# Six routed sequences' first products in pairs, as quarter products

## The chip, the cores and the metric

One core of a Trainium2 chip runs the kernel, as one program. The metric is the device time of one execution in microseconds, the median over several runs.

## The reference, cut to what matters

`x` has 8 sequences of 128 rows and 512 columns. Layer 0 adds an adapter product with a small LoRA mixture to it. Layer 1 computes attention over a paged cache (32 query heads, 8 key heads, head size 128, 512 cached keys and 128 new ones a sequence) and passes its output `y` through a routed product:

```python
scores = (y @ Wq_w.T) @ keys.T                    # 64 experts
top_vals, top_idx = top_k(scores, 16)
gate = scatter(softmax(top_vals))                 # 0 for the other 48
z = (y @ A_w.T).reshape(..., 64, 8)
x = x + ((z * gate[..., None]).reshape(..., 512) @ B_w.T) * SCALING
```

The change is in `y @ A_w.T` (512 x 512 a sequence), the scores and the gate.

## The kernel before, in words

Everything is fp32. Attention runs as 64 units (`NU = 64`; a unit is one key head with its four query heads `h` = 0 to 3, for one sequence), in the calls `iteration(u)`, u = 1 to 66, written out in order: the order in the code is each engine's order. The call `iteration(u)` handles several units at different stages: scores (PE, `s`, L439/L442) and exponential of unit u (DVE masks and takes the maximum, L452; ACT exponentiates, L463; DVE reciprocal, L468; POOL normalizes, L469; DVE transposes blocks, L474, L425 for the rotated queries and keys), a trip of these blocks through DRAM (`exchange_out`, `exchange_in`, tiles `px`, `pT`, `qkb`), the queries of unit u + 1 (ACT, `qkT`, L973), norms and rotation of unit u + 3 (ACT L311, POOL L315/L317, DVE L343), `values` of unit u - 2 (PE, `o`, L986), and `output` of unit u - 3 (PE, `y`, L1111 or L1124, after ACT's copy `oT`, L1009, which `evict_o` makes at the top of the call). DVE adds `y` up (L1180) and makes masks (L409).

After a sequence's last unit its routed product follows, in three steps. `f_turn` transposes `y` on PE (`ftp`, L858) and copies it (ACT, `yT`, L860). `f_project` (L867) multiplies it with the router and the weights side by side in `fw_t["sa"]`: `sz` (PE name `fr`) takes the 64 router columns and the first 256 of `A_w`, `z` (`fz`) the other 256, four 128-row chunks each; a call in fp32 is two instructions of the profile. The first lies in PSUM bank "q", the second in bank "kv". `f_gate` (L878 to L900) copies the scores out, finds the sixteen largest on DVE, exponentiates on ACT (L890), normalizes, and multiplies `z` by the gates from PSUM into `zg`. Sequences 0 to 6 do this at u = 59 to 65:

```python
LAST = {NU - 5 + b: b for b in range(B - 1)}
```

`f_turn` is called at h = 2 (h = 1 at u = 61, the top of the call from u = 64 on), `f_project` and `f_gate` at the end of the call, ahead of `values`; from u = 64 on `values` goes first (`ahead`). The gated `z` of sequences 0 to 5 is then block-transposed on DVE (`z_blocks`, L372), written to DRAM and read back turned (`z_exchange`, SP's queue, one sequence an iteration), copied (`z_turn`, ACT L393), and combined in pairs by POOL (`z_sums`). The second products, with `B_w`, are already made in pairs as seven quarter products (Winograd's form) behind the loop: `f_products`, PE `op` L1466, DVE additions L1477, and `f_store`. POOL makes the quarter sums of `B_w` in `f_quarters` (L934 to L937) at u = 64. `f_fold` (L850) folds weight columns at u = 59. `f_load_x` loads the rows of `x` that the output is added to. Sequence 7 is done behind the loop, and so are the last `z` turns.

PSUM has one bank each for "q", "kv", "o" and "y" and two double banks for scores.

Of the kernel before, what the change touches and what calls it, by code (L numbers as in the profile page):

```python
# [16 lines left out]
P = 128  # L17
# [41 lines left out]
def adaln_ffn_kernel(  # L59
# [816 lines left out]
    def f_gate(b, sz, z, sb, psum):  # L876
        sc = sb("sc", [P, E1])
        nc.vector.tensor_copy(sc, sz[:, :E1])  # L878
# [18 lines left out]
        nc.vector.tensor_scalar(wf, wf, den, SC1, ALU.mult, ALU.mult)  # L897
        zg = sb("zg", [P, DM])
# [29 lines left out]
    def f_quarters():  # L928
        b = fw_t["b"]
        q11, q12, q21, q22 = (b[:, 2 * i : 2 * i + 2, j * HN : (j + 1) * HN] for i in (0, 1) for j in (0, 1))  # L930
        room = [wo_t[:, i].rearrange("p (t c n) -> p t c n", t=2, c=2) for i in (3, 6)]
        t3, t2, t4, t1 = (room[i // 2][:, i % 2] for i in range(4))
        tt = nc.gpsimd.tensor_tensor
        tt(t3, q22, q12, ALU.subtract)  # L934
        tt(t2, t3, q11, ALU.add)
        tt(t4, q21, t2, ALU.subtract)
        tt(t1, q12, q11, ALU.subtract)  # L937
        fw_t["q"] = [q11, q21, q22, t4, t1, t2, t3]

    def z_sums(p):  # L940
        a, b = zT_t.pop(2 * p), zT_t.pop(2 * p + 1)
        at = p % 3 * 2 * DM
        room = spare[:, at : at + 2 * DM].rearrange("p (k c s) -> p k c s", k=4, c=2)
# [3 lines left out]
        tt(s1, a21, a22, ALU.add)  # L947
        tt(s2, s1, a11, ALU.subtract)
        tt(s4, a12, s2, ALU.subtract)
        tt(s3, a11, a21, ALU.subtract)  # L950
        zs_t[p] = [a11, a12, s4, a22, s1, s2, s3]
# [3 lines left out]
    with ExitStack() as l1:  # L955
# [276 lines left out]
        LAST = {NU - 5 + b: b for b in range(B - 1)}  # L1232
        yT_t, room_t = {}, {}

        def rooms():
            w = wp.tile([P, 7 * 2 * HW], F32, tag="wqkv", name="rooms", bufs=GH)
            at = [0]

            def part(size):
                at[0] += size  # L1240
                return w[:, at[0] - size : at[0]]

            for b in range(B - 1):
                room_t["zg", b] = part(DM)
            for i in range(2):
                room_t["yT", i] = part(DM)
                room_t["small", i] = part(352)

        def room(b):
# [9 lines left out]
            def psum(n, shape):  # L1259
                late = n == "tp" and b >= 5  # L1260
# [32 lines left out]

# [139 lines left out]
    with ExitStack() as l2:  # L1433
# [13 lines left out]
        def room4(z):  # L1447
            t = kvp.tile([P, 2 * DM], F32, tag="kt", name=f"fzT_{z}")
            return [t[:, i * DM : (i + 1) * DM].rearrange("p (c s) -> p c s", c=NC) for i in range(2)]

        M1, M2, M3, M4, M5, M6, M7 = range(7)
# [10 lines left out]
        def f_products(p, t, *which):  # L1462
            halves = [t[:, i * HN : (i + 1) * HN] for i in range(len(which))]
            for ps, n in zip(halves, which):
                for c in range(2):
                    nc.tensor.matmul(  # L1466
                        out=ps,
                        lhsT=zs_t[p][n][:, c, :],
                        rhs=fw_t["q"][n][:, c, :],
                        start=(c == 0),  # L1470
                        stop=(c == 1),
                    )
# [27 lines left out]
        end(0)  # L1500
        z_sums(2)
# [102 lines left out]
```

## Time and profile before

| | us |
|---|---|
| three runs | 1200.83, 1204.02, 1205.5 |
| median | 1204.02 |
| the profiled execution | 1200.24 |
| its span | 1198.5 |
| unit 59 starts (first `s`) | 1049.68 |
| units 60, 61, 62, 63 | 1066.35, 1086.23, 1100.89, 1120.69 |
| calls 64 and 65 and 66 start on PE | 1137.9, 1149.6, 1161.8 |
| first second product (`op`) | 1165.3 |
| last matmul ends | 1194.8 |

The granted TensorE clock of the execution is 1.000. In a row of the profile the engine is followed by the line of the kernel, the operation, the tile written and the tiles read (buffer numbers left out), shapes, and in brackets how long the engine idled before and what released it. PE is TensorE's matmuls, PEld its weight loads, DVE VectorE, ACT ScalarE, POOL GpSimd, SP SyncE.

### The profile page before, as it was taken

The page shows a single profiled execution, that of the slowest core. Times are in us where ns is not written, and L with a number is a line of the kernel's source. Part 1 is how long each engine was busy: PE and PEld are TensorE (multiplying, and loading weights), DVE is VectorE, ACT ScalarE, POOL GpSimd, SP SyncE. Part 2 cuts the span into 40 slices and gives each one's busy share as a digit, 9 for nine tenths or more (in the row PEclk, how much of TensorE's full clock was granted, in tenths as well). Part 3 has the DMA queues.
Part 4 walks back from the last instruction along what each step waited for, and adds up shares of the span by engine and source line. Part 5 has one row for each costly group of instructions (what it writes and reads, how often), then busy time and mean ns, then how long its engine had stood idle before and what let it go on. Part 6 is the DMA issues. An engine that isn't in the chain of part 4 may idle for free.

```text
span 1198.5 us, 16919 instructions
## 1 busy us (share of the span) xinstructions
PE 1189.8 (99%) x4196; PEld 723.0 (60%) x4196; DVE 927.0 (77%) x2122; ACT 504.2 (42%) x1457; POOL 755.1 (63%) x848
## 2 busy tenths in 40 slices
PE   9999999999999999999999999999999999999998
PEld 7666555565555556555556555555655555655557
DVE  2557788787888887878887787879888888887727
ACT  1345544443444444444444444444444444443310
POOL 3544779778845776678656685687657684653311
PEclk9999999999999999999999999999999999999999
DMA  8823787888888979898789978897889887888751
GB/s 317 304 83 114 249 247 242 261 274 261 263 255 254 315 236 284 262 292 287 246 257 285 291 232 283 286 287 251 285 237 308 266 252 246 277 281 243 230 176 71
DMA packets 205446, 302.34 MB, mean 252 GB/s; under 512 B 84771, under 2 KB 119332, under 8 KB 204324
## 3 DMA queue, kind: packets, MB, share of 16 engines
q1 hardware_dynamic: 170164, 196.29, 53.6%
q10 hardware_dynamic: 18864, 52.57, 13.7%
q0 software_dynamic: 16320, 52.40, 12.5%
q8 instruction: 34, 0.56, 0.2%
q14 instruction: 64, 0.52, 0.1%
HBM read 185.44 MB, written 115.74 MB: 251 GB/s over the span
## 4 chain that ended last, share of the span: by engine, by line
PE 91%; DVE 2%; POOL 2%; DMA 2%; ACT 1%; issue 1%; SPq 0%; ACTq 0%; DVEq 0%; POOLq 0%
PE o L986 20%; PE p L262 19%; PE s L439 17%; PE y L1111 13%; PE s L442 4%; PE p L295 3%; PE cp L627 2%; PE y L1124 2%; PE bp L649 2%; PE fr L867 1%; PE op L1466 1%; PE fz L867 1%; DVE xo L1477 1%; DMA qkb<-px 1%; ACT sq L311 1%
## 5 line engine op out<-in xcount | busy, mean ns | idle before, releaser
L463 ACT ACTIVATE p<-p,low 128x640 f32<-128x640 f32 x256 | 211.8, 828 | 430.6 <-DVE den L468 270.3
L469 POOL TENSOR_SCALAR p<-p,den 128x640 f32<-128x640 f32 x256 | 210.5, 823 | 231.9 <-DVE den L468 231.1
L452 DVE CUSTOM_DVE_ANT_0 p<-s,mask,rs 128x640 f32<-128x640 f32 x256 | 222.5, 879 | 86.9 <-PE s L442 85.2
L262 PE MATMUL p<-wqkv,xo 128*128 128x384 f32 x784 | 281.0, 487 | 0.1
L439 PE MATMUL s<-kt,qkT 128*128 128x512 f32 x504 | 258.1, 593 | 2.7 <-ACT oT L1009 1.9
L986 PE MATMUL o<-pT,vt 128*128 128x512 f32 x512 | 230.2, 592 | 0.0
L474 DVE STREAM_TRANSPOSE pb<-p 128x640 f32<-128x640 f32 x248 | 204.7, 826 | 21.5 <-POOL p L469 21.3
L1111 PE MATMUL y<-wo,oT 128*128 128x256 f32 x784 | 206.5, 380 | 0.5 <-DVE yp L1198 0.4
L262 PEld LDWEIGHTS p<-wqkv,xo 128*128 128x128 f32 x784 | 148.3, 190 | 69.2 <-POOL wqkv L163 0.9
L442 PEld LDWEIGHTS s<-qkT 128*128 128x128 f32 x504 | 95.8, 190 | 120.5 <-issue 120.5
L203 POOL DMA_INDIRECT vt<-in_vc,vrow x128 | 137.9, 1077 | 41.4 <-issue 31.5
L986 PEld LDWEIGHTS o<-pT,vt 128*128 128x128 f32 x512 | 97.2, 190 | 107.9 <-issue 92.8
L439 PEld LDWEIGHTS s<-kt,qkT 128*128 128x128 f32 x504 | 94.8, 190 | 74.6 <-issue 30.7
L1111 PEld LDWEIGHTS y<-wo,oT 128*128 128x128 f32 x784 | 131.8, 191 | 9.4 <-PE s L442 0.6
L311 ACT ACTIVATE sq<-c 128x128 f32<-128x128 f32 x320 | 98.8, 309 | 9.7 <-DVE oT L474 1.4
L442 PE MATMUL s<-qkT 128*128 128x128 f32 x504 | 96.8, 274 | 0.0
L317 POOL TENSOR_TENSOR rs<-ss,mhalf 128x5 f32<-128x5 f32 x64 | 82.4, 1287 | 5.3
L1009 ACT COPY oT<-o 128x512 f32<-128x512 f32 x64 | 37.4, 585 | 103.8 <-PE o L986 79.9
L315 POOL TENSOR_SCALAR ss<-ss,eps 128x5 f32<-128x5 f32 x64 | 24.7, 387 | 72.4 <-ACT sq L311 72.4
L986 PE MATMUL o<-pT,vn 128*128 128x512 f32 x128 | 65.4, 592 | 0.0
L265 DVE TENSOR_TENSOR c<-c,p 128x384 f32<-128x384 f32 x84 | 44.9, 534 | 24.1 <-PE p L262 23.8
L425 DVE STREAM_TRANSPOSE pb<-ca 128x640 f32<-128x640 f32 x60 | 50.1, 836 | 16.5 <-DMA kt<-in_kc 12.6
(255 smaller groups left out, 1481.2 us busy)
## 6 DMA issues: line engine op xcount, KB each, us to landing
pT<-px SPq DMA_DIRECT2D x64, 1280.0 KB
px<-pb SPq DMA_DIRECT2D x120, 400.0 KB
px<-pb ACTq DMA_DIRECT2D x120, 400.0 KB
qkb<-px SPq DMA_DIRECT2D x60, 320.0 KB
kt<-in_kc SPq DMA_DIRECT2D x512, 32.0 KB
wqkv<-in_wqkv POOLq DMA_DIRECT2D x32, 384.0 KB, 5.1
wo<-in_wo POOLq DMA_DIRECT2D x17, 512.0 KB, 7.7
yd<-yp POOLq DMA_DIRECT2D x12, 512.0 KB, 8.8
```

The lines of the kernel that those rows point to most:

```text
L203: nc.gpsimd.indirect_dma_start(out=kv_t[step][1][:, c, :], out_offset=None, in_=vc, in_offset=bass.IndirectOffsetOnAxis(ap=vrow[:, hf, at ...
L262: nc.tensor.matmul(out=ps, lhsT=xo[:, pr, x, c, :], rhs=w[:, c, :], start=(c == 0), stop=(c == 1))
L311: nc.scalar.activation(sq, cs[:, at : at + D], AF.Square, accum_out=ss[:, h : h + 1])
L317: nc.gpsimd.tensor_tensor(rs, ss, mhalf, ALU.pow)
L439: nc.tensor.matmul(out=s[:, :L], lhsT=qkT[:, h, :], rhs=kt[:, :, g % GH, :], start=True, stop=True)
L442: nc.tensor.matmul(out=s[:, L:NK], lhsT=qkT[:, h, :], rhs=qkT[:, REP, :], start=True, stop=True)
L452: nc.vector.tensor_tensor_reduce(out=p, in0=s_t.pop((u, h))[:, :NK], in1=mask_t[st], scale=rs_t[u][:, h : h + 1], scalar=BIG, op0=ALU.add, ...
L463: nc.scalar.activation(p, p, AF.Exp, bias=low, scale=-1.0, accum_out=den)
L469: nc.gpsimd.tensor_scalar(p_t[u, h], p_t[u, h], den, 1.0, ALU.mult, ALU.mult)
L474: nc.vector.transpose(pb_t[u][:, :, h * w : (h + 1) * w].rearrange("p i (j a) -> p j i a", a=32), p_t.pop((u, h)).rearrange("p (j i a) -> ...
L986: nc.tensor.matmul(out=o, lhsT=vt[:, c, j * D : (j + 1) * D] if c < LC else vn_t.pop(u), rhs=pT[:, c], start=(c == 0), stop=(c == LC),)
L1111: nc.tensor.matmul(out=y_t["y"][:, half * HN : (half + 1) * HN], lhsT=part(key)[:, i * S : (i + 1) * S], rhs=wo_t[:, slot(w, key[0] // (B ...
```

## The change

Sequences 0 to 5 are taken in the pairs (0,1), (2,3), (4,5). The 256 x 512 rows of a pair (two sequences' `yT`) times `A_w` become seven products M1 to M7 of quarters, each 128 rows by 256 columns with two 128-row chunks. The quarter sums of `A_w` are made once by four POOL steps of 128x512 (`qa_steps`, u = 59 and 60), those of `yT` by four POOL steps of 128x256 a pair (`f_step`). M1 and M2, which need only the even sequence, are made at the end of u = 59, 62, 64 (`FIRST`) and carry 64 router columns each, whose sum is the even sequence's scores; ACT copies their `z` part out (`m1`, `m2`) and the even gate is made. The rest is made at u = 61, 63, 65 (`REST`): M4, which carries router columns that hold one half of the odd sequence's scores, and a 64-column product `own_r` with the other half into the same bank, at h = 3; then M5, M6, M3, M7 at the end. M1 and M5 with M6 use bank "q"; M2, M4 with `own_r`, and M3 with M7 use bank "kv". At u = 62, 64, 66 (`GATED`) `f_add` puts the products together with six DVE adds of 256 columns, `f_mult` multiplies both sequences' `z` by the gates (two DVE steps of 128x512), and the pair's blocks are transposed; the exchange goes out one iteration later and back in after another. `f_turn` of the even sequences moves to behind h = 3 (u = 59, 62) or the top (u = 64), of the odd ones to h = 1 or the top (u = 65). Sequence 6 keeps the old form and moves from u = 65 to u = 66. `values` goes first from u = 63 on. The quarter sums of `B_w` use other rooms, `f_load_x` moves to u = 66 and behind the loop, and the last two `z` turns follow `end(0)`.

```diff
-    def f_gate(b, sz, z, sb, psum):
+    def f_scores(r, sb):
         sc = sb("sc", [P, E1])
-        nc.vector.tensor_copy(sc, sz[:, :E1])
+        nc.vector.tensor_copy(sc, r[0])
+        for more in r[1:]:
+            nc.vector.tensor_tensor(sc, sc, more, ALU.add)
+        return sc
...
+    def quarters_of(m, *rooms):
+        q11, q12, q21, q22 = (m[:, 2 * i : 2 * i + 2, j * HN : (j + 1) * HN] for i in (0, 1) for j in (0, 1))
+        t3, t2, t4, t1 = rooms
         tt = nc.gpsimd.tensor_tensor
...
+        steps = [
+            lambda: tt(t3, q22, q12, ALU.subtract),
+            lambda: tt(t2, t3, q11, ALU.add),
+            lambda: tt(t4, q21, t2, ALU.subtract),
+            lambda: tt(t1, q12, q11, ALU.subtract),
+        ]
+        return [q11, q21, q22, t4, t1, t2, t3], steps
...
+    def sums_of(a, b, room):
+        room = room.rearrange("p (k c s) -> p k c s", k=4, c=2)
         s1, s2, s3, s4 = (room[:, i] for i in range(4))
         a11, a12, a21, a22 = a[:, :2], a[:, 2:], b[:, :2], b[:, 2:]
...
+        steps = [
+            lambda: tt(s1, a21, a22, ALU.add),
+            lambda: tt(s2, s1, a11, ALU.subtract),
+            lambda: tt(s4, a12, s2, ALU.subtract),
+            lambda: tt(s3, a11, a21, ALU.subtract),
+        ]
+        return [a11, a12, s4, a22, s1, s2, s3], steps
...
+    def quarter_products(t, left, right, *which):
+        halves = []
+        at = 0
+        for n in which:
+            halves.append(t[:, at : at + right[n].shape[2]])
+            at += right[n].shape[2]
+        for ps, n in zip(halves, which):
+            for c in range(2):
+                nc.tensor.matmul(
+                    out=ps,
+                    lhsT=left[n][:, c, :],
+                    rhs=right[n][:, c, :],
+                    start=(c == 0),
+                    stop=(c == 1),
+                )
+        return halves
...
-        LAST = {NU - 5 + b: b for b in range(B - 1)}
+        LAST = {NU + 2: B - 2}
+        FIRST = {NU - 5: 0, NU - 2: 1, NU: 2}
+        REST = {NU - 3: 0, NU - 1: 1, NU + 1: 2}
+        GATED = {NU - 2: 0, NU: 1, NU + 2: 2}
...
-        def z_blocks(b):
-            if 0 <= b < TURNED:
-                turn_blocks(zg_t[b], spare[:, b * DM : (b + 1) * DM])
-
-        def z_exchange(b):
-
-            if 0 <= b < TURNED:
-                written_t[b] = turn_out(b, spare[:, b * DM : (b + 1) * DM])
-            if 0 <= b - 1 < TURNED:
-                turn_in(written_t.pop(b - 1), zg_t[b - 1])
+        def z_blocks(u):
+            if u in GATED:
+                for b in (2 * GATED[u], 2 * GATED[u] + 1):
+                    turn_blocks(zg_t[b], spare[:, b * DM : (b + 1) * DM])
+
+        def z_exchange(u):
+            for back, do in ((1, "out"), (2, "in")):
+                if u - back in GATED:
+                    for b in (2 * GATED[u - back], 2 * GATED[u - back] + 1):
+                        if do == "out":
+                            written_t[b] = turn_out(b, spare[:, b * DM : (b + 1) * DM])
+                        else:
+                            turn_in(written_t.pop(b), zg_t[b])
...
+        fs_room, t1_room, m1, m2, m4, u2, u3, m35 = (own(n) for n in (2 * DM, DM, *[HN] * 6))
+        fs_t, sc_t, sb_t, wf_t, ps_t, steps_t = {}, {}, {}, {}, {}, {}
+
+        def f_turn_of(b):
+            yT_t[b] = f_turn(b, *room(b))
+
+        def f_first_products(p):
+            b = 2 * p
+            yT = yT_t[b]
+            left, right = [yT[:, :2], yT[:, 2:]], fw_t["qa"]
+            (one,) = quarter_products(bank("q", f"fq_{b}"), left, right, M1)
+            (two,) = quarter_products(bank("kv", f"fr_{b}"), left, right, M2)
+            nc.scalar.copy(m1, one[:, E1:])
+            nc.scalar.copy(m2, two[:, E1:])
+            sb = room(b)[0]
+            wf_t[b] = f_weights_of(f_scores([one[:, :E1], two[:, :E1]], sb), sb)
+
+        def f_step(p, *which):
+            if p not in steps_t:
+                fs_t[p], steps_t[p] = sums_of(yT_t[2 * p], yT_t[2 * p + 1], fs_room)
+            for i in which:
+                steps_t[p][i]()
+
+        def f_both(p):
+            return [room_t["zg", 2 * p + i] for i in range(2)], w_zg[:, 2 * p * DM : (2 * p + 2) * DM].rearrange(
+                "p (k n) -> p k n", k=4
+            )
+
+        def f_rest_products(p, part):
+            left, right = fs_t[p], fw_t["qa"]
+            b = 2 * p + 1
+            if part == 0:
+                t = bank("kv", f"fk_{p}")
+                (four,) = quarter_products(t, left, right, M4)
...
+                own_r = t[:, E1 + HN : 2 * E1 + HN]
+                for c in range(2):
+                    nc.tensor.matmul(
+                        out=own_r, lhsT=yT_t[b][:, c, :], rhs=fw_t["s"][:, c], start=(c == 0), stop=(c == 1)
+                    )
+                nc.scalar.copy(m4, four[:, E1:])
+                nc.gpsimd.tensor_tensor(f_both(p)[1][:, 0], m1, m2, ALU.add)
+                sb_t[b] = room(b)[0]
+                sc_t[b] = f_scores([four[:, :E1], own_r], sb_t[b])
+            else:
+                ps_t[p] = [
+                    *quarter_products(bank("q", f"fm_{p}"), left, right, M5, M6),
+                    *quarter_products(bank("kv", f"fn_{p}"), left, right, M3, M7),
+                ]
+                wf_t[b] = f_weights_of(sc_t.pop(b), sb_t.pop(b))
+
+        def f_add(p):
+            m5, m6, m3, m7 = ps_t.pop(p)
+            z = f_both(p)[1]
+            tt = nc.vector.tensor_tensor
+            tt(u2, m1, m6, ALU.add)
+            nc.scalar.copy(m35, m5)
+            tt(u3, u2, m7, ALU.add)
+            tt(z[:, 1], u2, m3, ALU.add)
+            tt(z[:, 2], u3, m4, ALU.add)
+            tt(z[:, 1], z[:, 1], m35, ALU.add)
+            tt(z[:, 3], u3, m35, ALU.add)
+
+        def f_mult(p):
+            for b, zg in zip((2 * p, 2 * p + 1), f_both(p)[0]):
+                v = zg.rearrange("p (e r) -> p e r", r=R1)
+                nc.vector.tensor_tensor(v, v, wf_t.pop(b).unsqueeze(2).to_broadcast([P, E1, R1]), ALU.mult)
+                zg_t[b] = zg
+
+        qa_steps = []
+        room2 = None
+
+        def f_room(tag):
+            t = kvp.tile([P, 2 * DM], F32, tag=tag, name=f"f_{tag}", bufs=3 if tag == "vt" else None)
+            return [t[:, i * DM : (i + 1) * DM].rearrange("p (c s) -> p c s", c=NC) for i in range(2)]
         def iteration(u):
+            nonlocal room2
             on = lambda v: 0 <= v < NU
             fb = LAST.get(u)
...
                 load_whole(NQ * B - 4 + u - NU + 5)
-            z_exchange(u - NU + 3)
+            z_exchange(u)
             if on(u - 3):
                 evict_o(u - 3)
-            if u >= NU and fb is not None:
+            if u == NU + 2:
+                f_add(2)
+                for b in range(4):
+                    f_load_x(b)
+            if fb is not None:
                 yT_t[fb] = f_turn(fb, *f)
+            if u == NU:
+                f_turn_of(2 * FIRST[u])
+            elif u == NU + 1:
+                f_turn_of(2 * REST[u] + 1)
+                f_step(REST[u], 0, 1, 2, 3)
+            if u == NU + 1:
+                room2 = f_room("kt")
             if u > NU:
-                z = u - NU - 1
-                z_turn(z, wo_t[:, slot(T4, NQ - 1), z * DM : (z + 1) * DM].rearrange("p (c s) -> p c s", c=NC))
-                for b in range(4 * z, 4 * z + 4):
-                    f_load_x(b)
-            if u >= NU:
-                z_blocks(u - NU + 4)
+                z_turn(u - NU - 1, room2[u - NU - 1])
+            if u == NU + 2:
+                f_mult(2)
+                z_blocks(u)
             if u == NU:
-                f_quarters()
+                fw_t["q"], steps = quarters_of(
+                    fw_t["b"],
+                    *quarter_rooms(wo_t[:, 3]),
+                    *quarter_rooms(kvp.tile([P, 2 * DM], F32, tag="vt", name="f_quarters", bufs=3)),
+                )
+                for do in steps:
+                    do()
             if u in (2, 3):
                 norms(u + 3)
             for h in range(REP):
...
                         f_fold()
+                    if u == NU - 5 and h == 1:
+                        t4 = wo_t[:, 6, : 2 * (E1 + HN)].rearrange("p (c n) -> p c n", c=2)
+                        fw_t["qa"], qa_steps[:] = quarters_of(
+                            fw_t["a"],
+                            *quarter_rooms(wo_t[:, 5]),
+                            t4[:, :, E1:],
+                            t1_room.rearrange("p (c n) -> p c n", c=2),
+                        )
+                        sa = fw_t["sa"]
+                        fw_t["qa"][M1], fw_t["qa"][M2] = (sa[:, c : c + 2, : E1 + HN] for c in (0, 2))
+                        fw_t["qa"][M4] = t4
+                    at = (u - NU + 5, h)
+                    if at == (1, 0):
+                        nc.vector.tensor_copy(fw_t["qa"][M4][:, :, :E1], fw_t["s"][:, 2:])
+                    if at in ((0, 1), (0, 2), (1, 0), (1, 1)):
+                        qa_steps.pop(0)()
+                    if u in GATED and h == 1:
+                        f_add(GATED[u])
+                    if u in GATED and h == 2:
+                        f_mult(GATED[u])
                     if h == 3:
-                        z_blocks(u - NU + 4)
-                    if h == (1 if u == NU - 3 else 2) and fb is not None:
-                        yT_t[fb] = f_turn(fb, *f)
+                        z_blocks(u)
+                        if u in FIRST:
+                            f_turn_of(2 * FIRST[u])
+                    if u in REST:
+                        if h == 1:
+                            f_turn_of(2 * REST[u] + 1)
+                        elif h > 1:
+                            f_step(REST[u], 2 * h - 4, 2 * h - 3)
+                elif u in GATED and u < NU + 2:
+                    if h == 1:
+                        f_add(GATED[u])
+                    elif h == 2:
+                        f_mult(GATED[u])
+                    elif h == 3:
+                        z_blocks(u)
                 if on(u - 3):
                     output(u - 3, h)
                     sums_a(u - 3, h)
+                if u in REST and h == 3:
+                    f_rest_products(REST[u], 0)
                 if h > 0 and slots:
                     project(k, j, slots[h - 1 : h])
...
-            ahead = u >= NU
+            ahead = u >= NU - 1
             if ahead and on(u - 2):
                 values(u - 2)
+            if u in FIRST:
+                f_first_products(FIRST[u])
+            if u in REST:
+                f_rest_products(REST[u], 1)
             if fb is not None:
                 f_gate(fb, *f_project(fb, yT_t.pop(fb), *f), *f)
             if not ahead and on(u - 2):
...
-        z_exchange(TURNED)
+        z_exchange(NU + 3)
+        z_exchange(NU + 4)
+        for b in range(4, B):
+            f_load_x(b)
         z_sums(0)
-        for p in (1, 2):
-            for b, zT in zip((2 * p, 2 * p + 1), room4(p)):
-                z_turn(b, zT)
+        for b, zT in zip((2, 3), f_room("kt")):
+            z_turn(b, zT)
         z_sums(1)
         begin(0)
         yT = f_turn(b7, sb, psum)
         end(0)
+        for b, zT in zip((4, 5), f_room("vt")):
+            z_turn(b, zT)
         z_sums(2)
         ps = f_project(b7, yT, sb, psum)
         f_gate(b7, *ps, sb, psum)
```

More of the change, by code (lines that the diff above doesn't have):

```diff
@@ L874, in f_project, with f_weights_of @@
         return sz, z
-    def f_gate(b, sz, z, sb, psum):
+    def f_scores(r, sb):
         sc = sb("sc", [P, E1])
-        nc.vector.tensor_copy(sc, sz[:, :E1])
+        nc.vector.tensor_copy(sc, r[0])
+        for more in r[1:]:
+            nc.vector.tensor_tensor(sc, sc, more, ALU.add)
+        return sc
+    def f_weights_of(sc, sb):
         top = sb("top", [P, 8])
@@ L897, in f_gate @@
         nc.vector.tensor_scalar(wf, wf, den, SC1, ALU.mult, ALU.mult)
+        return wf
+    def f_gate(b, sz, z, sb, psum):
+        wf = f_weights_of(f_scores([sz[:, :E1]], sb), sb)
         zg = sb("zg", [P, DM])
@@ L926, in f_load_x, with quarter_rooms @@
         nc.sync.dma_start(out=x1_t[b], in_=x1_d[ORDER[b]])
[L928 to L932, printed above, removed]
-        tt = nc.gpsimd.tensor_tensor
[L934 to L943, printed above, removed]
+    def quarters_of(m, *rooms):
+        q11, q12, q21, q22 = (m[:, 2 * i : 2 * i + 2, j * HN : (j + 1) * HN] for i in (0, 1) for j in (0, 1))
+        t3, t2, t4, t1 = rooms
+        tt = nc.gpsimd.tensor_tensor
+        steps = [
[5 more added lines that the diff above has]
+        return [q11, q21, q22, t4, t1, t2, t3], steps
+    def quarter_rooms(t):
+        return [t[:, i * DM : (i + 1) * DM].rearrange("p (c n) -> p c n", c=2) for i in range(2)]
+    def sums_of(a, b, room):
+        room = room.rearrange("p (k c s) -> p k c s", k=4, c=2)
         s1, s2, s3, s4 = (room[:, i] for i in range(4))
@@ L946, in z_sums @@
         tt = nc.gpsimd.tensor_tensor
[L947 to L951, printed above, removed]
+        steps = [
[5 more added lines that the diff above has]
+        return [a11, a12, s4, a22, s1, s2, s3], steps
+    def z_sums(p):
+        at = p % 3 * 2 * DM
+        zs_t[p], steps = sums_of(zT_t.pop(2 * p), zT_t.pop(2 * p + 1), spare[:, at : at + 2 * DM])
+        for do in steps:
+            do()
+    M1, M2, M3, M4, M5, M6, M7 = range(7)
+    def quarter_products(t, left, right, *which):
[14 more added lines that the diff above has]
+        return halves
     spare = xo.rearrange("p r x c s -> p (r x c s)")
@@ L1228, in load_whole @@
             ya_t[st] = t
-        LAST = {NU - 5 + b: b for b in range(B - 1)}
+        LAST = {NU + 2: B - 2}
+        FIRST = {NU - 5: 0, NU - 2: 1, NU: 2}
+        REST = {NU - 3: 0, NU - 1: 1, NU + 1: 2}
+        GATED = {NU - 2: 0, NU: 1, NU + 2: 2}
         yT_t, room_t = {}, {}
+        w_zg = None
         def rooms():
+            nonlocal w_zg
             w = wp.tile([P, 7 * 2 * HW], F32, tag="wqkv", name="rooms", bufs=GH)
@@ L1244, in rooms @@
                 room_t["zg", b] = part(DM)
+            w_zg = w[:, : (B - 1) * DM]
             for i in range(2):
@@ L1259, in psum @@
             def psum(n, shape):
-                late = n == "tp" and b >= 5
+                late = n == "tp" and b >= 4
                 t = banks(f"ftp_{b}") if late else bank("kv" if n == "z" else "q", f"f{n}_{b}")
@@ new lines, in z_exchange, with own @@
+        def z_exchange(u):
[6 more added lines that the diff above has]
+                            turn_in(written_t.pop(b), zg_t[b])
+        def own(size, at=[spare.shape[1]]):
+            at[0] -= size
+            return spare[:, at[0] : at[0] + size]
@@ L1328, in iteration @@
                 load_whole(NQ * B - 4 + u - NU + 5)
-            z_exchange(u - NU + 3)
+            z_exchange(u)
             if on(u - 3):
                 evict_o(u - 3)
-            if u >= NU and fb is not None:
-                yT_t[fb] = f_turn(fb, *f)
-            if u > NU:
-                z = u - NU - 1
-                z_turn(z, wo_t[:, slot(T4, NQ - 1), z * DM : (z + 1) * DM].rearrange("p (c s) -> p c s", c=NC))
-                for b in range(4 * z, 4 * z + 4):
-                    f_load_x(b)
-            if u >= NU:
-                z_blocks(u - NU + 4)
-            if u == NU:
-                f_quarters()
+            if u == NU + 2:
[3 more added lines that the diff above has]
+            if fb is not None:
+                yT_t[fb] = f_turn(fb, *f)
+            if u == NU:
[5 more added lines that the diff above has]
+                room2 = f_room("kt")
+            if u > NU:
+                z_turn(u - NU - 1, room2[u - NU - 1])
+            if u == NU + 2:
+                f_mult(2)
+                z_blocks(u)
+            if u == NU:
+                fw_t["q"], steps = quarters_of(
[3 more added lines that the diff above has]
+                )
+                for do in steps:
+                    do()
             if u in (2, 3):
@@ L1445, in psum @@
             return t[:, : shape[1]] if len(shape) == 2 else t.rearrange("p (c s) -> p c s", c=NC)
[L1447 to L1451, printed above, removed]
         INTO = {
@@ L1462, in f_products @@
         def f_products(p, t, *which):
[L1463 to L1472, printed above, removed]
+            halves = quarter_products(t, zs_t[p], fw_t["q"], *which)
             x1 = spare[:, (TURNED + 2 * p) * DM : (TURNED + 2 * p + 2) * DM]
```

## The prediction

> **What bounds the kernel now.** I read the page first: section 1 for the share of each engine, section 2 for where in the span one is idle.
>
> ```profile
> PE 1189.8 (99%) x4196; PEld 723.0 (60%) x4196; DVE 927.0 (77%) x2122; ACT 504.2 (42%) x1457; POOL 755.1 (63%) x848
> ...
> PE   9999999999999999999999999999999999999998
> ```
>
> PE is busy for 1189.8 of 1198.5 us and full in every slice but the last. A matmul taken out shortens the span by its own length; a wait put in front of PE lengthens it by its own length. DVE at 77% has slack on average, but only in pieces. Next the chain of waits from 1049 us on. It is PE for nearly the whole stretch; these lines carry one sequence's first product and what surrounds it:
>
> ```profile
> 1112.68 2.15 PE fr L867 x8
> 1114.84 1.73 PE fz L867 x8
> 1116.56 4.29 PE o L986 x10
> ...
> 1137.26 0.59 ACT oT L1009
> 1137.86 0.04 issue
> 1137.90 3.70 PE y L1124 x8
> ```
>
> So eight 320-column instructions (two to a call) take 2.15 us, 0.27 each, and eight of 256 columns 1.73, 0.216 each: a sequence costs 3.88 us of PE. The last three lines show the kind of wait that matters: `y` cannot start before ACT has copied `oT`. The windows by stage say how much PE idles where the change works:
>
> ```profile
> 1049.68:1066.35 16.67, 16.56 (x63) 10.67 (x62) 14.10 (x31) 7.67 (x22) 10.34 (x13) 1.00 0.97 314
> ...
> 1120.69:1137.90 17.21, 16.97 (x60) 9.63 (x58) 12.60 (x33) 5.73 (x13) 8.21 (x8) 1.00 0.66 208
> ```
>
> These are units 59 and 63 (columns: length, then PE, PEld, DVE, ACT, POOL, clock, DMA share, GB/s). PE idles 0.11 and 0.24 us; by instruction starts the waits of before that the change can swallow are 0.28 us at 1066.35, 0.40 around 1137.9 (0.24 of it named as a wait for oT) and 0.20 near 1161.8, together 0.9.
>
> **What is saved on PE.** Two sequences cost 2 x 3.88 = 7.76 us. As quarter products: M1 and M2, two calls of 320 columns each, 8 instructions x 0.27 = 2.16; M4 likewise 1.08; M5, M6, M3, M7, 16 x 0.216 = 3.46. Added: `own_r`, two calls of 64 columns, 4 instructions. By columns they cost 4 x 0.054 = 0.22; by the transposes (`ftp`, four 128-column instructions in 0.44) at most 0.44. I take 0.44, since a call of so few columns brings new weights each time, as a transpose does. Sum 7.14, saved 0.62 a pair, 1.9 us in all (1.6 to 2.5). Transposes and everything else on PE keep their number.
>
> **What is added on PE as waiting.** Before, each product had its yT copy (L860) made at h = 2, one head ahead, and its gate ran long after. The change moves the copy behind the exponential of h = 3 in units 59 and 62, and makes second products wait for PSUM banks. ACT and DVE take their instructions in order, so I read their timelines:
>
> ```profile
> 1057.04 0.56 ACT L860 COPY rooms<-ftp 128x512 f32<-128x512 f32 x1
> 1059.13 0.84 ACT L463 ACTIVATE p<-p,low 128x640 f32<-128x640 f32 x1 [1.53 <-DVE den L468]
> ...
> 1095.40 0.83 ACT L463 ACTIVATE p<-p,low 128x640 f32<-128x640 f32 x1 [1.65 <-DVE den L468]
> ...
> 1111.99 0.83 ACT L463 ACTIVATE p<-p,low 128x640 f32<-128x640 f32 x1 [1.84 <-DVE den L468]
> ...
> 1148.85 0.35 ACT L890 ACTIVATE rooms<-rooms 128x64 f32<-128x64 f32 x1 [10.52 <-DVE rooms L882]
> 1149.11 0.56 ACT L1009 COPY oT<-o 128x512 f32<-128x512 f32 x1
> ```
>
> Unit 59: PE reaches the product at 1057.90, unchanged, as the transposes only move within the unit. The exponential of h = 3 starts at 1059.13 because DVE's mask step for it comes late (1058.14), behind the fold copy L850 (1.52 us) and two block transposes. The exponential ends 1059.97, the copy 1060.53, PE starts near 1060.6: a hole of 2.7 us. Low end 2.3 (DVE starts 0.4 earlier), high end 3.9 (second rival).
>
> Unit 61: M4 starts when s of h = 3 ends, 6.65 us into the unit. With M4, own_r, M5 and M6, PE would be ready for M3 at 6.65 + 1.08 + 0.44 + 1.73 = 9.9, and at 10.05 counting M5's wait for POOL's first sum (normalization of h = 1 done at 7.5, 0.73 for a 128x256 sum, 0.1 to pass it on). But M3 takes the bank that M4 and own_r stand in, and that is free only after ACT's m4 copy and DVE's copy and add of the scores. The exponential of h = 3 (1095.40, 9.17 into the unit) frees ACT at 10.0; the m4 copy of 256 columns is 0.37 (between 0.26 for 128 and 0.46 for 384); then 0.1 to 0.2, and two DVE steps of 0.23: 11.1. The hole is 1.05 there and 0.15 to 0.25 before M5, 1.3 (0.9 to 1.6). In unit 63 the same products are cheap to place: `values` is now ahead of them (4.3 us), while POOL's four sums (2.9 us) and the copies finish. Nothing is late.
>
> Unit 62: the exponential of h = 3 started 1111.99 and let ACT go at 1112.82; the copy moved behind it ends 1113.4, and PE's product came at 1112.52 before: 0.9 late even with DVE on time. DVE has 3.8 us of idle gaps between the four mask steps of this unit (0.57, 1.83, 1.36), and gets six adds of 0.42 (2.5) and two 128x512 multiplies of 0.68 (1.4): 3.9. They just fit, pushing the last step by some 0.25. The hole is 1.15 (0.6 to 1.7).
>
> Unit 65: `y` waits for oT of unit 62. ACT's queue has m1, m2, the gate's Exp (L890) and then this oT copy. From the end of M2: m2 copied at 0.5; scores copied and added, maximum and its negative (0.23, 0.23, 0.15 with 0.04 to 0.2 between them) at 1.45; Exp, next ACT step 0.26 later; oT 0.56: ready at 2.2. Of before, PE had fz (1.73) and ftp (0.44) to do meanwhile; now ftp alone. The hole is 1.75 (1.5 to 2.0).
>
> The other moves cost nothing where I find cover. The odd gates start behind values or the next unit's scores. DVE loses twelve multiplies of 0.42 (L900) and gets six of 0.68 and eighteen adds of 0.42, 6.6 us more in all; outside unit 62 they lie in calls 64 and 66, where DVE was busy for 2.4 of 11.7 us (window of call 64). SP's queue gets each pair's eight transfers out one unit, in the next, instead of four and four every unit; the first z rows are needed at 1165 us, 40 us after they leave, and pair 2's (out behind the loop) only for op_2, more than 5 us after they land; if that cover went, op_2 would be late by what is missing. f_load_x for sequences 4 to 7 stands behind them on SP; its rows too are wanted only by the closing additions. The 33 us from the first `op` to the end are PE-bound and keep their work. POOL's four subtractions for qa (1.27 us each) lie in units 59 and 60, where POOL idles for 5 and 9 us.
>
> **A rule against it.** The clock was 1.00 in all windows of before, with no gap of PE inside the span over 1.37 us; it fell to half some 3.4 us after the last matmul, which two windows at the end show:
>
> ```profile
> 1194.90:1198.20 3.30, 0.00 (x0) 0.00 (x0) 0.78 (x2) 0.00 (x0) 0.00 (x0) 1.00 0.45 159
> 1198.20:1198.50 0.30, 0.00 (x0) 0.00 (x0) 0.00 (x0) 0.00 (x0) 0.00 (x0) 0.63 0.00 0
> ```
>
> So a 2.7 us hole leaves the clock alone. [...]
>
> **The sum.** Holes 2.7 + 1.3 + 1.15 + 1.75 = 6.9; less the 0.9 of old waits, which they swallow, and the 1.9 saved: +4.1. On the profiled execution's own time, 1200.24 us, that is 1204.3; this execution lies 3.8 below the median of the three runs, 1204.02, so the median should come to 1208.1, 0.34% slower. By the bounds: holes 5.3 to 9.2, less 0.9, less 1.6 to 2.5: +1.9 to +6.7, so 1205.9 to 1210.7. A difference of 0.5%, 6.0 us, is about what a measurement of this kernel can tell from no change.
>
> **Rivals.** *The holes close* (ACT or DVE get to the copies early because every unit behind a hole has more slack): only the saving is left, with some of the old waits, -1.9 to -2.8, 1201.7. Against it: in unit 59 nothing precedes that could give DVE slack, so 2.7 us at least partly stands. Chance 0.07.
>
> *POOL holds DVE back* and the change is slower beyond the bound. Before shows the mechanism in unit 63, where DVE steps of a gate stand beside POOL's subtractions:
>
> ```profile
> 1134.13 1.27 POOL L936 TENSOR_TENSOR wo<-fw,wo 128x512 f32<-128x512 f32 x1
> 1134.24 1.24 DVE L893 TENSOR_TENSOR rooms<-rooms 128x64 f32<-128x64 f32 x1
> ```
>
> The same DVE step takes 0.22 to 0.23 alone; here it ends with POOL's instruction. The change puts such POOL work where DVE sets the hole: in unit 59 the first subtraction follows straight on the normalization that the fold copy already sits out, so the copy may lose up to 1.2 more; in units 61 and 63 sums of 0.73 stand beside the score additions, and later gates. Two or three such hits on the path are 1.9 to 2.7 us: +6.0 to +6.8, 1210.4. It decides from 1.9 us. For it: the gate's next earlier step met a subtraction too and took 0.41 for 0.23; against it: mask steps and block transposes keep their 0.88 and 0.82 beside POOL's normalizations. Chance 0.31.
>
> *The columns are not saved*: own_r and the doubled changes of bank and weights eat the 0.62 a pair. Then +4.1 + 1.9 = +6.0, 1210.0. The uniform 0.27 and 0.216 in the chain speak against it. Chance 0.05.
>
> **How the numbers follow.** My own case has 0.55, of which 0.09 lies over 6.0 us (its bound is 6.7, and a wait that I missed adds to it); the first rival is within 0.5%, the second slower, the third half of each; 0.02 remains for a gain that I can't name, since the whole saving with all the old waits is only 2.8 us. Slower 0.09 + 0.31 + 0.02 = 0.42; faster 0.02; same 0.46 + 0.07 + 0.03 = 0.56. The range reaches from the first rival's upper end, 1202, over the second with the spread of the runs (median to highest 1.5, lowest 3.2 below), to 1215.
>
> **What would show it.** In the profile after: PE gaps of 2.7, 1.3, 1.15 and 1.75 us in units 59, 61, 62 and 65, released by ACT's yT copy, the bank of M4, the yT copy and oT; fq and fr at 1.08 each, own_r at 0.44. A yT copy of unit 59 that ends before 1058 would make me wrong downwards; L850 longer than 2 us, a clock below 1.00, or DVE mask steps that delay `s`, upwards.

## The result and the profile after

The changed kernel takes 1210.37 us (median of seven runs, 1206.64 to 1213.87) against 1201.2 for the kernel before (seven runs, 1199.33 to 1205.5): ratio 1.0073, interval 1.0057 to 1.0089, slower. Timed again, unaltered, beside other kernels it had 1.0050 (1.0030 to 1.0069). The profiled execution has a span of 1209.3 us. The page's lines that answer to those shown of before:

```profile
PE 1190.6 (98%) x4196; PEld 721.6 (60%) x4196; DVE 938.0 (78%) x2141; ACT 508.3 (42%) x1469; POOL 773.9 (64%) x867
...
PE   9999999999999999999999999999999999989998
```

One slice near the end has dropped to 8: there PE waits. That PE's busy time rose by 0.8 although columns were taken out says that some matmuls ran slower.

For all comparisons I use a stretch of PE's timeline: from the first scores of unit 59 to the first second product (`op`). It was 115.6 us (1049.68 to 1165.31) and is 122.3 (1053.87 to 1176.14), 6.6 more. From `op` to the last matmul both take 29.53. The rest of the difference of the two spans, 4.2 us, stands ahead of unit 59, where the two programs are alike; I come back to it with the first experiment.

The waits of PE from 1045 to 1180 us (us in total, times, longest), which were one of 0.2 us before:

```profile
PE fq L981 <- ACT rooms L860: 4.1, 2, 3.4
PE y L1161 <- ACT oT L1046: 1.7, 1, 1.7
PE fn L981 <- ACT qkT L1010: 0.8, 1, 0.8
```

In PE's timeline they have their places (in brackets the idle time before the row; `fr`, `fk` and `o` shown for their durations):

```profile
1065.64 1.65 PE L981 MATMUL fq<-fw,rooms 128*128 128x320 f32 x4 [3.39 <-ACT rooms L860]
1067.08 2.34 PE L981 MATMUL fr<-fw,rooms 128*128 128x320 f32 x4
...
1096.93 0.55 PE L1378 MATMUL fk<-fw,rooms 128*128 128x64 f32 x4
...
1100.37 1.10 PE L981 MATMUL fn<-fw,xo 128*128 128x256 f32 x4 [0.80 <-ACT qkT L1010]
...
1118.95 1.34 PE L981 MATMUL fq<-fw,rooms 128*128 128x320 f32 x4 [0.69 <-ACT rooms L860]
1120.13 1.24 PE L981 MATMUL fr<-fw,rooms 128*128 128x320 f32 x4
...
1155.58 3.70 PE L1161 MATMUL y<-wo,oT 128*128 128x512 f32 x8 [1.70 <-ACT oT L1046]
```

The four forecast holes are there, in units 59, 61, 62 and call 65. (`fn` is put down to `qkT`, the last event before it; by the code it waits for the bank that M4 and `own_r` stand in, and DVE's last step on that bank is this, which ends 0.15 us ahead of `fn`:)

```profile
1100.00 0.22 DVE L880 TENSOR_TENSOR rooms<-rooms,fk 128x64 f32<-128x64 f32 x1
```

The two rows `fr` differ: 2.34 in unit 59, 1.24 in unit 62, for the same columns. The windows just after the first hole say why (the clock is the third number from the end):

```profile
1065.64:1066.50 0.86, 0.86 (x3) 0.68 (x4) 0.86 (x3) 0.86 (x3) 0.65 (x1) 1.00 1.00 396
1066.50:1068.00 1.50, 1.50 (x4) 1.01 (x3) 1.32 (x3) 1.37 (x8) 0.15 (x1) 0.52 1.10 353
1068.00:1069.42 1.42, 1.42 (x4) 0.88 (x3) 1.30 (x3) 0.54 (x3) 1.00 (x1) 0.50 0.87 203
```

The clock was halved for 3.4 us from 1066.5 on. By the chain of waits fq, fr and o took 1.65, 2.13 and 4.62 us there instead of 1.08, 1.08 and 4.29: 1.95 us. Not all of this is the clock: behind the hole in unit 62, at full clock, fq took 1.34, so the slow clock alone cost about 1.7. And the hole is longer than 2.7 because of what DVE and POOL did in h = 1 of the unit (the first line is from the kernel before, the others from the changed one):

```profile
1053.80 1.52 DVE L850 COPY fw<-fw 128x256 f32<-128x256 f32 x1
...
1057.98 2.74 DVE L850 COPY fw<-fw 128x256 f32<-128x256 f32 x1
...
1058.52 0.81 POOL L469 TENSOR_SCALAR p<-p,den 128x640 f32<-128x640 f32 x1
1059.30 1.26 POOL L942 TENSOR_TENSOR wo<-fw 128x512 f32<-128x512 f32 x1
1060.65 0.87 DVE L452 CUSTOM_DVE_ANT_0 p<-s,mask,rs 128x640 f32<-128x640 f32 x1
```

The fold copy ends 0.16 us behind POOL's new subtraction and takes 1.22 us longer than before, and DVE's mask step comes after it.

### The profile page after: what moved, and what is told of

It reads as the page before. It is cut to its first block, busy times and chain, and to the rows that moved or that the text cites. A ratio compares the mean times of both kernels' runs of the same rounds, so it can differ in the third digit from the quotient of the medians.

```text
span 1209.3 us, 17007 instructions
## 1 busy us (share of the span) xinstructions
PE 1190.6 (98%) x4196; PEld 721.6 (60%) x4196; DVE 938.0 (78%) x2141; ACT 508.3 (42%) x1469; POOL 773.9 (64%) x867
## 4 chain that ended last, share of the span: by engine, by line
PE 84%; DVE 4%; DMA 4%; POOL 3%; issue 2%; ACT 2%; SPq 1%; ACTq 0%; DVEq 0%; POOLq 0%
PE o L1023 19%; PE p L262 18%; PE s L439 16%; PE y L1148 12%; PE s L442 4%; PE p L295 3%; PE cp L627 2%; PE bp L649 2%; PE y L1161 2%; DMA kt<-in_kc 1%; DMA px<-pb 1%; DVE pb L474 1%; PE op L981 1%; POOL p L469 1%; SPq L192 1%
## 5 line engine op out<-in xcount | busy, mean ns | idle before, releaser
L315 POOL TENSOR_SCALAR ss<-ss,eps 128x5 f32<-128x5 f32 x64 | 27.3, 427 | 76.8 <-ACT sq L311 76.8
L425 DVE STREAM_TRANSPOSE pb<-ca 128x640 f32<-128x640 f32 x60 | 50.2, 836 | 15.7 <-DMA kt<-in_kc 10.4
```

## Experiments

My theory: the excess of 6.6 us is four waits of PE (in unit 59 3.55 by the chain, of which the row above shows 3.39 as idle, 1.4 in unit 61, 0.95 in unit 62, 1.95 in call 65) and 1.95 of halved clock, less 2.0 saved and some 1.1 of old waits that they swallow. (With 1.7 for the clock, as above, and the 0.9 of the prediction for the old waits the sum is the same 6.6 to 6.7; the expectations go by 1.95.) The rivals stand in the expectations. The table has, for each profile, the start of unit 59, the stretch, the hole ahead of the first product of unit 59, whether the clock halved after it, and the ratio to the kernel before.

| kernel | start | stretch | hole | clock | ratio (interval) |
|---|---|---|---|---|---|
| before | 1049.7 | 115.6 | none | 1 | 1 |
| changed | 1053.9 | 122.3 | 3.39 | half | 1.0073 (1.0057 to 1.0089) |
| changed, again | 1050.6 | 122.1 | 3.38 | half | 1.0050 (1.0030 to 1.0069) |
| subtractions later | 1050.1 | 119.8 | 2.64 | 1 | 1.0035 (1.0020 to 1.0050) |
| the same, second execution | 1052.5 | 121.6 | 2.71 | half | one profile only |
| filler | 1052.8 | 120.7 | 2.52 | 1 | 1.0049 (1.0032 to 1.0067) |
| early turn | 1053.6 | 118.6 | 0.84 | 1 | 1.0027 (1.0014 to 1.0040) |
| oT first | 1050.2 | 120.3 | 3.39 | half | 1.0052 (1.0033 to 1.0071) |
| values first | 1055.3 | 122.2 | 3.40 | half | 1.0050 (1.0030 to 1.0069) |
| before, late turn | 1048.8 | 120.3 | 2.46 | half | 1.0046 (1.0029 to 1.0062) |
| the same, second execution | 1051.9 | 120.1 | 2.54 | half | one profile only |
| before, one subtraction | 1054.0 | 116.4 | 0.83 | 1 | 1.0011 (0.9998 to 1.0024) |
| all four treated | 1050.5 | 114.7 | none | 1 | 0.9991 (0.9970 to 1.0012) |
| the same, subtractions spread | 1054.4 | 114.1 | none | 1 | 0.9983 (0.9966 to 0.9999) |

**The changed kernel again.** No edit.

> The changed kernel once more, unaltered. My theory: 6.8 of its excess lie between the first scores of unit 59 and the first second product (122.4 us in the changed kernel's profile, 115.6 in the one of before), and the 4.2 us by which unit 59 starts later are mostly chance of the run. Then this profile shows 122 to 123 again for that stretch, and a start of unit 59 anywhere from 1048 to 1055. Rival: the change also slows what comes before unit 59; then the start is at 1053 to 1055 again.

The stretch came out at 122.1 again and unit 59 started at 1050.6, 3.3 us earlier. Over all profiles of the table the start lies between 1048.8 and 1055.3, for kernels made from before (1048.8 to 1054.0) as for those made from the changed one (1050.1 to 1055.3). So the 4.2 us ahead of unit 59 in the first pair of profiles are mostly chance; the means of the two groups, four and ten profiles, are 1.3 us apart, so a fixed part of about that size can't be excluded.

**POOL's subtractions a head later.**

```diff
-if at in ((0, 1), (0, 2), (1, 0), (1, 1)):
+if at in ((0, 2), (0, 3), (1, 0), (1, 1)):
     qa_steps.pop(0)()
```

> The four subtractions of POOL for qa come one head later each (h = 2 and 3 of unit 59, 0 and 1 of unit 60), so that none follows the normalization behind which the fold copy waits. My theory (POOL holds the fold copy 1.2 us longer, the hole of PE so passes the length at which the clock halves): L850 falls from 2.74 to about 1.5, the hole from 3.4 to 2.2-2.7, the clock stays at 1.00, and the stretch from unit 59 to the first second product falls by 3.2 us (1.2 of hole, 1.95 of clock). Rival (the clock falls for another reason): 1.2 us less, fq and fr still 1.65 and 2.13. Rival (the copy is long for its own reason): nothing moves.

L850 took 1.50 us, and PE's hole was shorter:

```profile
1054.21 1.50 DVE L850 COPY fw<-fw 128x256 f32<-128x256 f32 x1
...
1061.12 1.34 PE L981 MATMUL fq<-fw,rooms 128*128 128x320 f32 x4 [2.64 <-ACT rooms L860]
```

So what held the copy was the subtraction behind the normalization; without it the hole is 2.64, by the chain 2.8, near the 2.7 of the prediction. The clock stayed at 1.00 and the stretch fell by 2.4 (0.75 of hole, 1.7 of clock); I had expected 3.2, because I counted the clock at 1.95 and the copy's 1.22 in full, while the block transpose L425 now waited 0.40 for a transfer of the exchange.

> The kernel with the later subtractions once more (hole 2.64, clock 1.00 the first time). If the clock looks at windows that run freely beside the program, a hole of this length may halve it in one run and not in the next; if a length decides, the clock stays at 1.00 again and something else made it fall in the other kernel.

The second execution of this kernel went the other way: a hole of 2.71, and then (windows)

```profile
1063.62:1064.60 0.98, 0.98 (x4) 0.74 (x5) 0.98 (x2) 0.95 (x4) 0.66 (x1) 1.00 1.03 400
1064.60:1067.60 3.00, 3.00 (x7) 1.87 (x6) 2.81 (x7) 1.83 (x9) 1.98 (x3) 0.50 0.88 289
```

The clock halved one microsecond after PE had resumed, and the stretch was 121.6. One program, two executions with nearly the same hole, one with and one without: the length of the hole alone doesn't decide. What does is worked out below, under the late turn.

**A filler in the hole.**

```diff
+if p == 0:
+    idle = bank("kv", "idle_f")
+    for _ in range(8):
+        nc.tensor.transpose(idle[:, :S], ident, ident)
 (one,) = quarter_products(bank("q", f"fq_{b}"), left, right, M1)
```

> Eight transposes of the identity into the idle bank kv stand ahead of the first product of unit 59 (0.9 us of PE work that nobody reads). They take no time from anyone, but break PE's idle stretch of 3.4 us into one of 2.5. My theory (the idle length makes the clock fall): L850 stays at 2.7, the product starts where it started, fq, fr and o run at 1.08, 1.08 and 4.29, and the stretch is 1.95 us shorter. Rival (the clock falls because of the transfers or of what PE did before): fq and fr stay slow and nothing moves.

The copy took 2.75 us, the idle stretch was 2.52, and the clock stayed:

```profile
1064.58 1.34 PE L981 MATMUL fq<-fw,rooms 128*128 128x320 f32 x4 [2.52 <-ACT rooms L860]
1065.76 1.24 PE L981 MATMUL fr<-fw,rooms 128*128 128x320 f32 x4
```

1.24 for `fr` instead of 2.34, and 1.4 to 1.6 us off the stretch. The transfers and the data are those of the changed kernel, so they alone don't make `fr` slow. That the filler did it can't be shown by one execution, since a hole of 2.46 to 2.71 us was followed by the half clock in some executions only. Over the runs the gain isn't seen (1.0049). The mean clock that is on record for each run says why. A half clock of 3.4 us takes 0.0014 off the mean, and the mean was 0.998 or less in four of the filler's twelve runs, in five of the changed kernel's thirteen and in none of the early turn's twelve (in three of 77 of the kernel before): the filler hardly made the slow clock rarer.

**The turn back at h = 2, in unit 59 alone.**

```diff
 if h == 3:
...
-    if u in FIRST:
+    if u in FIRST and not (u == NU - 5):
         f_turn_of(2 * FIRST[u])
+if h == 2 and u in FIRST and (u == NU - 5):
+    f_turn_of(2 * FIRST[u])
```

> In unit 59 alone the transposes and the yT copy of sequence 0 go back to h = 2. My theory: the copy then ends behind the exponential of h = 2 (62.4 + 0.6 in the changed kernel's time, 1063.05), PE is ready at 1062.1, so a hole of about 0.95 is left, the clock stays at 1.00, and the stretch is 4.5 us shorter (2.6 of hole, 1.95 of clock). Rival (DVE's lateness passes to PE in another way, through the scores' banks or the blocks): the hole moves into unit 60 and less than 3 us are gained.

The hole was 0.84, the clock 1.00, unit 59 took 15.8 instead of 20.0 us. Of these 4.2 us unit 60 gave 0.6 back, so that the stretch fell by 3.6, of 4.5 expected: PE waited there for a bank of the scores.

```profile
1072.12 1.29 POOL L944 TENSOR_TENSOR wo<-fw,wo 128x512 f32<-128x512 f32 x1
1072.78 0.73 DVE L897 TENSOR_TENSOR rooms<-rooms 128x64 f32<-128x64 f32 x1
...
1074.49 0.88 DVE L452 CUSTOM_DVE_ANT_0 p<-s,mask,rs 128x640 f32<-128x640 f32 x1
...
1075.43 1.12 PE L439 MATMUL s<-kt,qkT 128*128 128x512 f32 x2 [0.35 <-DVE low L452]
```

The gate of sequence 0, with a step held by another subtraction (0.73 for 0.23), keeps DVE from the first mask step. In the changed kernel this gate began 1.7 us before the scores of unit 60 (1072.14, 1073.88), here 1.6 us behind them (1070.97, 1069.32): the long hole had covered it.

**oT ahead of the gate.**

```diff
-if on(u - 3):
+if on(u - 3) and u != NU + 1:
     evict_o(u - 3)
...
+if p == 2:
+    evict_o(NU - 2)
 nc.scalar.copy(m1, one[:, E1:])
```

> Of the changed kernel one thing is altered: ACT copies oT of unit 62 at the end of call 64, ahead of the m1 and m2 copies and of the gate's Exp, not behind them at the top of call 65. My theory: o of unit 62 is done 2.2 us before M2 is, so oT is ready before PE gets to y; the hole of 1.70 in call 65 is gone, nothing else is late, and the stretch from unit 59 to the first second product is 1.7 to 2.0 us shorter (120.2 to 120.5 of 122.2). Rival: m1 and m2 come later, the gate of sequence 4 with them, and y or the next products wait for a bank instead: under 0.8 us gained.

The second half stands in `f_first_products`. From unit 63 to `op` it took 48.67 instead of 50.64 us: 1.97 gained. PE's rows now follow each other:

```profile
1149.61 0.60 PE L858 MATMUL ftp<-ident,ya 128*128 128x128 f32 x4
1150.04 3.60 PE L1161 MATMUL y<-wo,oT 128*128 128x512 f32 x8
```

The hole was the order of ACT's queue. Over the runs the gain isn't seen (1.0052 against 1.0050, and each interval is over 4 us wide).

**Values first in unit 61.**

```diff
-ahead = u >= NU - 1
+ahead = u >= NU - 1 or u == NU - 3
```

> Of the changed kernel one thing is altered: in unit 61 the values of unit 59 (4.3 us of PE) go between M4 and the other four products, as they do in unit 63. My theory: the wait of M3 and M7 for the bank of M4 (0.8) and for POOL's sums (0.6 in pieces) is then covered, since the exchange of unit 59 has landed by then; unit 61 falls from 17.1 to 15.75 us and the stretch by 1.35. Rival: the products' end, now right before unit 62, holds up f_add and the mask steps there; the hole moves into unit 62 and under 0.5 us is gained.

Unit 61 fell from 17.10 to 15.76 us, 1.34, and unit 62 kept its 19.03. The stretch did not fall, since unit 59 took 21.3 us in this execution, 1.3 more: its clock was halved for 6.8 us instead of 3.4, of which PE worked through these:

```profile
1067.12:1073.10 5.98, 5.98 (x10) 3.54 (x11) 4.38 (x10) 3.52 (x14) 3.00 (x3) 0.50 0.98 282
```

**Before with the late turn alone.**

```diff
-if h == (1 if u == NU - 3 else 2) and fb is not None:
+if h == (1 if u == NU - 3 else 3 if u in (NU - 5, NU - 2) else 2) and fb is not None:
     yT_t[fb] = f_turn(fb, *f)
```

> The kernel of before, with one part of the change alone: in units 59 and 62 transposes and yT copy come at h = 3 instead of h = 2. My theory (order of ACT's queue makes the hole, and below 3.4 us the clock does not react): holes of 2.65 in unit 59 and 0.9 in unit 62, clock 1.00, the stretch from 115.6 to 118.9 us. Rival (the holes come from the new work on DVE and POOL): the stretch stays within 0.7 us of 115.6.

The holes came, 2.46 and 0.32 us, without any of the new products. But the clock fell, after 2.46 us of idle time:

```profile
1059.59 4.11 PE L867 MATMUL fr<-fw,rooms 128*128 128x320 f32 x8 [2.46 <-ACT rooms L860]
```

4.11 instead of 2.32: the stretch grew by 4.6, not 3.3. So the order makes the hole of unit 59, as I had held, and my limit for the clock was wrong. In unit 62 it makes only part: 0.32 us here, of 0.9 expected, and 0.69 in the changed kernel, where DVE's mask step of h = 3 also comes 0.40 us later in the unit (10.07 against 9.67).

> The kernel of before with the late turn once more (hole 2.45, clock halved for 3.6 us the first time). With freely running windows: hole again 2.45, clock either way, unit 59 at 20.8 or near 19.0 us. If this kernel's work decides: halved again, 20.8.

The second execution repeated it: hole 2.54, clock halved, stretch 120.1.

When the clock changes, the traces tell exactly. In the changed kernel it is halved at 1066.545 and back at 1069.958 us, and it falls again behind the last matmul, 41 times 3.413 us later. In each of the fourteen traces all entries of the clock record lie whole multiples of 3.413 us apart (in the changed kernel 311 from the first entry to the halving, then 1 and 41; in the kernel before 349 between its two). So in these traces the clock changed only at the marks of a grid of 3.413 us that kept its step through the hole and the work on both sides of it. I call the stretch between two marks a window, and the holes of the table can be laid against these windows:

| execution | hole | window with most of it | PE idle in it | clock after it |
|---|---|---|---|---|
| oT first | 3.39 | 1058.63 to 1062.04 | 3.34 | half |
| changed, again | 3.38 | 1058.61 to 1062.03 | 3.06 | half |
| values first | 3.40 | 1062.90 to 1066.31 | 2.59 | half, two windows |
| changed | 3.39 | 1063.13 to 1066.55 | 2.51 | half |
| before, late turn | 2.46 | 1056.59 to 1060.00 | 2.46 | half |
| subtractions later, second execution | 2.71 | 1061.20 to 1064.62 | 2.42 | half |
| before, late turn, second execution | 2.54 | 1059.04 to 1062.46 | 2.14 | half |
| filler | 2.52 | 1060.45 to 1063.86 | 1.79 | 1 |
| subtractions later | 2.64 | 1056.39 to 1059.81 | 1.33 | 1 |

The idle time within one window orders all nine: the clock fell from 2.14 us on and stayed up to 1.79. The chance is where a hole lies against the windows: the hole of 2.64 was cut into 1.33 and 1.31, that of 2.71 fell into one window with 2.42. In values first the window at half clock held another 0.81 us of idle time, and a second one followed. One window at half clock cost 1.5 to 1.7 us: from the first product of unit 59 to the scores of unit 60 the changed kernel took 8.06 to 8.24 us with it and 6.54 or 6.55 without, the kernel before 9.75 and 9.97 against 8.27. Two windows cost 3.0 (9.51).

**Before with one subtraction.**

```diff
 f_fold()
+a = fw_t["a"]
+nc.gpsimd.tensor_tensor(
+    room_t["zg", 5].rearrange("p (c n) -> p c n", c=2),
+    a[:, 2:, HN:], a[:, :2, HN:], ALU.subtract,
+)
```

> The kernel of before, with one POOL subtraction of 128x512 added at h = 1 of unit 59, right behind the fold copy, into a room that nobody reads. My theory (POOL holds the copy): L850 from 1.52 to 2.74; the exponential of h = 2 and the yT copy behind it 1.2 later, 1058.85 in the time of before against PE ready at 1057.90: a hole of 0.95, the stretch 0.7 longer (an old wait of 0.28 goes). Rival (what PE and ACT do then makes the copy long): L850 stays at 1.5 and the stretch at 115.6.

```profile
1058.08 2.75 DVE L850 COPY fw<-fw 128x256 f32<-128x256 f32 x1
...
1063.18 1.07 PE L867 MATMUL fr<-fw,rooms 128*128 128x320 f32 x3 [0.83 <-ACT rooms L860]
```

The one POOL instruction lengthened this DVE copy by 1.23 us (2.75 for 1.52), and this passed through the mask step, the exponential and the yT copy to PE: stretch 116.4, 0.73 longer, near the 0.7 worked out.

**All four holes treated.** Four edits of the changed kernel together (subtractions later, early turn, oT first, values first), with the early turn in unit 62 as well.

> All four holes of the changed kernel are treated at once: POOL's subtractions one head later, transposes and yT copies of sequences 0 and 2 back at h = 2, oT of unit 62 copied ahead of the gate, values first in unit 61. My theory (the saving on PE is real and only waits ate it): no gap of PE over 0.4 us, clock 1.00, the stretch from unit 59 to the first second product 112.6 to 113.5 us, against 115.6 of before and 122.2 of the changed kernel; ratio to before 0.998. Rival (each closed hole opens another one, in the scores' banks of units 60 and 62 above all): the stretch stays over 115.6.

The four holes were gone, but the stretch was 114.65, not 112.6 to 113.5: PE waited 1.17 us for a load of `kt` in unit 60 and 0.33 for a mask step. Ratio 0.9991 (0.9970 to 1.0012), no difference that the runs can tell.

**The same with the subtractions spread,** at `((0, 2), (1, 1), (1, 2), (1, 3))`.

> As the one with all four holes treated, but POOL's last three subtractions stand at h = 1, 2 and 3 of unit 60. Theory: the first gate's step L897, which POOL held for 0.5 us at the start of unit 60, is free again, and the wait of s for the mask step there (0.35 with the early turn alone) is gone: 0.3 to 0.6 us less than its sister. Rival (the gate itself, 3 us on DVE ahead of the mask step, makes that wait): the same as its sister within 0.1.

The waits of PE from 1045 to 1175 us:

```profile
PE s L439 <- DVE low L452: 0.6, 1, 0.6
PE s L439 <- issue: 0.2, 1, 0.2
```

The wait for the mask step remained, although L897 took its 0.23 us again. So no held step is needed for it, and the rival was right on the cause: the gate, begun 2.5 us behind the unit's first scores, is enough. The stretch of 114.1 is 0.5 below its sister's all the same, because the load's wait of 1.17 is gone in this execution and the mask step's is only 0.26 longer. This version has the lowest ratio of all, 0.9983 (0.9966 to 0.9999), but the interval barely leaves out 1 and overlaps its sister's. In the stretch it is 1.5 us below the kernel before, of 2.0 that were taken off PE.

## Why the prediction was right and where it was short

The direction, the places and the range were right; the size and the odds were not. Worked out were 4.1 us, and the same stretch shows 6.6 in the two first profiles. The prediction put 0.56 on a difference within 0.5% and 0.42 on slower; it came out at 0.73%, and at 0.50% when timed again. That the median, 1210.37, lies only 2.3 us from the forecast of 1208.1 is partly luck: the forecast starts from the three runs' median of 1204.02, while seven runs of the same kernel have 1201.2. It is luck too that 6.6 lies just under the 6.7 of its upper bound, since that bound has no slow clock in it. By the steps:

- The saving: 1.9 forecast, 2.0 measured. M1, M2 and M4 take 1.08 each; `own_r` 0.39 to 0.41, near the upper end of its bounds: close to the 0.44 of four transposes (`ftp`), not the 0.22 of its columns. The third rival is out.
- Unit 61: 1.3 forecast, 1.4 measured (1.34 given back by values first). Unit 62: 1.15 forecast, 0.95 measured. Call 65: 1.75 forecast, 1.97 given back by oT first.
- Unit 59 is the term that was mis-sized: 2.7 forecast, 3.55 measured. The 2.7 was right for a copy that the new subtraction doesn't hold, as the later subtractions showed (2.64 idle, 2.8 by the chain). The second rival's first place was hit: 1.22 us of one held DVE instruction. Its other places, the sums in units 61 and 63, didn't reach PE. With this one hit alone the rival would not have decided.
- The larger miss is the clock, which the sum had at nothing: I had held that a hole of 2.7 us leaves it alone. The half clock came with 3.4 in four of four executions, and in three of five with 2.46 to 2.71. In the profile of the changed kernel it cost about 1.7 us, and 4.1 plus 0.85 plus 1.7 is the 6.6 measured. I took the limit from the fall 3.4 us after the last matmul of the kernel before; there the matmul happened to end (1194.84) just as a window began (1194.87), so the whole window was idle, while in the late turn's second execution 2.14 us of idle time in one were followed by the half clock too.
- Two of the prediction's three signs for a miss upwards came: L850 longer than 2 us (2.74), and a clock below 1.00.

In medians the change cost 9.2 us when first timed and 6.4 when timed again, against 6.6 in the profiles' stretch; I take the difference for the chance ahead of unit 59 and in the clock.

## What to carry to other kernels

Where one engine is full, work taken off it pays only if what feeds it stays ahead: here 2.0 us of columns were saved and some 9.6 us of waits and slow clock came in, most of it by the order of ACT's queue, the rest by a DVE copy that took 2.74 us instead of 1.52 beside one more POOL instruction, and by the clock. Before moving a step behind another in a queue, read when the step ahead of it really starts, and who on another engine may stretch it. And give a hole in TensorE's work a price for the clock as well: here the half clock followed seven of nine holes of 2.46 to 3.40 us, one window at half clock cost 1.5 to 1.7 us, and one program had a hole of 2.64 us without it and one of 2.71 with it.

## What the runs showed of the hardware

The clock halved after idle gaps of 2.46, 2.54 and 2.71 us and did not after 2.52 and 2.64 us; one and the same program did both. After gaps of 3.4 us it halved in four executions of four, for 3.41 us in three and 6.83 in one. In the fourteen traces all its changes lay whole multiples of 3.413 us apart. In the seven executions with the half clock PE had idled 2.14 to 3.34 us between two marks of this grid, in the two without it 1.33 and 1.79. The DVE copy L850 of 128x256, begun beside a POOL instruction, ended 0.15 to 0.16 us behind the last of POOL's instructions in a row and not between two of them: after 1.52 us (before) and 1.50 (subtractions later) with two POOL instructions beside it, the normalization last, after 2.74 (changed) and 2.75 (before, one subtraction) with a 128x512 subtraction behind them.
